# Layer 0's feed-forward for two entries between the state-space steps, C by DMA, sums over states by transposes, the last layer's second routing in front

## The chip, the cores and the metric

The kernel runs on one core of one Trainium2 chip. The metric is the device time of one execution in microseconds (us); lower is better. TensorE is written PE in profiles (PEld: its weight loads), VectorE DVE, ScalarE ACT, GpSimd POOL, SyncE SP. Before the change the median of three runs is 2589.24 us (2589.22 to 2589.57).

## The reference, cut to what matters

The reference is a decoder of four layers, each with self-attention, cross-attention and a feed-forward part, every part followed by a residual addition and a layer norm. There are four batch entries of 512 positions and 128 features, all in float32. The change touches three of the twelve parts:

```python
# L0_ffn: x is (4, 512, 128); _tlin multiplies by a matrix of -1, 0, 1 and scales
h = silu(_tlin(x, w1_w, w1_s)) * _tlin(x, w2_w, w2_s)      # 512 hidden features
h = gelu(_tlin(h, h1_w, h1_s), approximate=False)
h = gelu(_tlin(h, h2_w, h2_s), approximate=False)
return _tlin(h, w3_w, w3_s)                                # back to 128

# L1_attn: a selective state space, 256 inner features, 16 states
xi, z = split(x @ W_in);  xc = silu(conv4(xi) + conv_b)
dt, Bm, Cm = split(xc @ W_x, [8, 24])
delta = softplus(dt @ W_dt + b_dt);  A = -exp(A_log)
dA = exp(delta[..., None] * A);  dBu = delta[..., None] * Bm[:, :, None, :] * xc[..., None]
# over positions t: h = dA_t * h + dBu_t;  y_t = sum over the 16 states of h * C_t
return (y + xc * D) * silu(z) @ W_out

# L3_ffn: a shared expert for every row, and two of seven routed experts
probs = sigmoid(x @ Wr * routing_bias);  scores, idx = top_k(probs, 2)
out = shared(x) + sum over the two of (silu(x @ wg) * (x @ wu)) @ wd * score
```

## The kernel before

**The frame.** Each of the twelve parts is a generator that emits instructions and yields after every small piece. It has three phases: a start, up to the mark READY; a main phase, up to the mark TAIL; and a tail. While the main phase of a part runs, weights of the next part are loaded. Then the tail of the ending part (called "A") and the start of the next one (called "B"; for the parts in BESIDE also its first main pieces) are taken in turns, in an order written out by hand as a string of As and Bs in ORDER; when a string ends, the turns go on as "ABB". Nothing moves instructions after that: each engine does its instructions in the order in which they were emitted, and waits on semaphores for data and for buffers. So an instruction that waits holds up everything behind it on its engine.

**PSUM.** PSUM has a pool "s" of two tiles of two banks, and single banks "y", "v", "a0", "a1". A dictionary for each part and phase (RINGS: FORWARD for L0_ffn, STATES for L1_attn) says which of them a kind of use takes, in turn. A bank is free for its next writer when its last reader is done.

**L0_ffn** (from L1626). For each entry, `gates` does two matmuls of 128x512 for each of four chunks into a pair of banks; ACT applies silu, DVE multiplies the second result by its scale and by silu. `hidden` does four matmuls for each of four output chunks and a GELU on ACT, twice (layers h1 and h2). `output` does sixteen matmuls of 128x128, DVE multiplies by the scale, POOL adds the residual, and `finish_pieces` gives statistics (DVE, then two small POOL operations, L342 and L343), norm (DVE, L351) and the turning over into xT (four transposes, L359, and a copy). The start holds gates and h1 of entry 0. The main phase does everything else up to h1 of entry 3. The tail holds output of entry 2, h2 and output of entry 3, in turns with the start of L1_attn.

**L1_attn** (from L2284). The features lie on the 128 partitions in two halves c, positions along the row. `prepare(b)` gives the pieces for an entry: `convolved` (four shifted matmuls of 128x512 into pscv, silu to xc), `gates` (psz, silu to sz), `selected` (px, copied as bf16 to bc, with the remainders of the rounding in its other rows), `exponentials` (pdt, then seven ACT operations) and `logarithm` (five DVE operations for each half), and two POOL operations for de and du. Then there are 32 steps g, eight for an entry, each for NQ = 2 of the 16 states. In one step:

- `decays(g+1)`: four ACT exponentials, da (L2412)
- `spread(g+1, "B", c)`: PE spreads two rows of B over all partitions into pb, one tile of "s" for each half (L2398); `spread(g+1, "C", c)`: one matmul into pc (L2404), copied by ACT to cs (L2405)
- `recurred(g)`: for both halves DVE multiplies pb by du in place (L2423); then for each half DVE scans over positions (L2426) and POOL multiplies hh by cs (L2430)
- `summed(g-1, c)`: PE adds the two states into acc, a bank for each half that is kept over the entry's eight steps, by two matmuls with the identity (L2439)

The order in a step is recurred, decays, then for each half summed and spread. From step 1 of an entry on, the pieces of the next entry's `prepare` run one in each step (Agenda `early`, between summed(c=0) and spread(c=0)), and its logarithms in steps 4 and 5. `outputs` finishes an entry: DVE adds D times xc to acc (yt, L2448), POOL multiplies by sz, PE projects by W_out (yps) seven steps later, and residual, statistics and norm follow.

**L3_ffn** (from L1918). Rows are sorted to experts in two groups, entries 0 and 1 and entries 2 and 3. `routing(b)` computes the scores (plog, sigmoid, and some twenty small DVE operations), `ranked` and `numbered` the places, `placing` writes the rows to DRAM in that order by indirect DMA, `load` fetches them, two blocks at a time. The main loop goes over blocks q of 128 rows: `gates` (psgu, L2144), `hidden_over` (ph), `down` (py) and an indirect DMA out. The routing of entry 2 stands in front of the loop; that of entry 3, the ranks and the placing of the second group run inside it, by an agenda: 

```python
agenda.add(0, routing(3))
agenda.add(6, [lambda: ranked(1), lambda: None, lambda: numbered(1)])
for i, f in enumerate(placing(1)):
    agenda.add(9 + 3 * i // 4, [f])
```

## Time and profile before

| | us |
|---|---|
| median of the runs | 2589.24 |
| profiled execution | 2600.57 |
| its span on the engines | 2598.9 |
| first scan of L1_attn | 545.62 |
| start of its last two scans | 805.84 |
| first block of L3_ffn's loop on PE | 2454.50 |

The profiled execution is 11.3 us (0.44%) over the median, so a sum in its times has to be scaled before it is set beside a median. A row of a group or of a timeline gives the start, the busy time, the engine, the line in the kernel, what is written and read, and in brackets the idle time ahead of it with the instruction that ended it. In PE's rows the last part of a group can overlap the next row: a matmul is counted until its result has drained, so differences of starts give the pace. "PEclk" is the granted TensorE clock as a share of full speed; it is 0.954 over the whole span.

### The profile page before, as it was taken

The numbers are of one execution on the slowest core, as the hardware profiler recorded it, in microseconds if no ns is written. First come the engines' busy times: TensorE is split into PE (matmuls) and PEld (weight loads), VectorE is DVE, ScalarE is ACT, GpSimd is POOL, SyncE is SP. The second block draws the span as 40 slices with busy tenths as digits, with TensorE's granted clock in tenths as the row PEclk, the third lists the DMA queues.
The fourth block names the chain that finished last, engine by engine and source line by source line (L and its number), as shares of the span: only waits on it lengthen the run. The fifth ranks groups of instructions, "written<-read, shape, count | busy, mean of one in ns | idle before, by whom it ended". The sixth has DMA issues, their size and how long they took to land.

```text
span 2598.9 us, 37485 instructions
## 1 busy us (share of the span) xinstructions
PE 2310.4 (89%) x13754; PEld 1109.1 (43%) x13754; DVE 1681.9 (65%) x3028; ACT 1243.8 (48%) x2537; POOL 1138.3 (44%) x1545
## 2 busy tenths in 40 slices
PE   5998879988877998999999999999889799999887
PEld 1333334433333443444444555555445333344565
DVE  6896961179998666565554655655767699666434
ACT  2776432277652444333232455555354387745323
POOL 2342430157676325555552444344336434231354
PEclk7999899999988999999999999999899699999999
DMA  5422314000003400000000000000300243130112
GB/s 146 136 72 69 105 32 50 0 1 0 1 4 87 150 7 7 1 1 1 1 1 1 8 8 13 1 13 13 106 21 1 61 110 89 57 123 13 37 59 77
DMA packets 97415, 109.34 MB, mean 42 GB/s; under 512 B 30992, under 2 KB 82960, under 8 KB 97232
## 3 DMA queue, kind: packets, MB, share of 16 engines
q1 hardware_dynamic: 92592, 99.31, 13.8%
q0 software_dynamic: 2432, 5.02, 0.5%
q10 hardware_dynamic: 2208, 2.62, 0.3%
q8 instruction: 109, 1.79, 0.3%
q14 instruction: 74, 0.61, 0.1%
HBM read 68.94 MB, written 41.44 MB: 42 GB/s over the span
## 4 chain that ended last, share of the span: by engine, by line
PE 61%; DVE 16%; ACT 9%; POOL 5%; issue 4%; DMA 3%; SPq 1%; another core or an unknown queue 0%; POOLq 0%; ACTq 0%; DVEq 0%
PE av L714 4%; PE psve L1305 4%; PE scc L1142 4%; PE yT L1348 3%; PE avc L1215 3%; PE ptc L1202 3%; PE psh L1653 3%; ACT pr L1176 3%; PE sc L675 2%; DVE top L972 2%; PE avx L1000 2%; PE psqk L1487 2%; PE psgu L2144 2%; PE st L691 2%; DVE top L679 2%
## 5 line engine op out<-in xcount | busy, mean ns | idle before, releaser
L1186 POOL TENSOR_TENSOR pr<-pr,zs 128x1024 f32<-128x1024 f32 x192 | 237.1, 1252 | 238.8 <-DVE zs L1183 209.8
L679 DVE TENSOR_REDUCE top<-sc 128x2 f32<-128x1024 f32 x256 | 300.9, 1217 | 44.1 <-PE sc L675 41.4
L700 ACT ACTIVATE pT<-st 128x512 f32<-128x512 f32 x512 | 276.2, 598 | 88.3 <-PE st L691 85.1
L1176 ACT ACTIVATE pr<-scc,nm 128x256 f32<-128x256 f32 (+3 forms) x384 | 198.2, 526 | 179.5 <-DVE nm L1164 100.8
L972 DVE TENSOR_REDUCE top<-scx 128x4 f32<-128x616 f32 x256 | 192.2, 794 | 84.7 <-PE scx L959 73.5
L978 ACT ACTIVATE pTx<-stx 128x512 f32<-128x512 f32 x256 | 139.2, 596 | 201.4 <-PE scx L959 135.9
L497 POOL CAST nmP<-top 128x16 bf16<-128x16 f32 x96 | 25.4, 265 | 365.3 <-DVE top L972 203.6
L1164 DVE TENSOR_REDUCE nm<-scc 128x2 f32<-128x1024 f32 (+3 forms) x128 | 102.4, 821 | 120.1 <-PE scc L1149 120.1
L2430 POOL TENSOR_TENSOR hh<-hh,cs 128x1024 f32<-128x1024 f32 x64 | 149.3, 2354 | 65.9 <-DVE hh L2426 44.5
L714 PE MATMUL av<-pT,vbuf 128*32 128x256 f32 x2048 | 162.8, 392 | 8.9 <-ACT avs L514 8.9
L1310 DVE TENSOR_TENSOR vtmp<-psve,gm 128x1024 f32<-128x1024 f32 x64 | 78.3, 1224 | 130.7 <-PE psve L1305 130.6
L1142 PE MATMUL scc<-k,q 64*128 64x512 f32 (+3 forms) x768 | 143.4, 471 | 7.4 <-DVE vtmp L1310 3.3
L2426 DVE TENSOR_TENSOR_SCAN hh<-da,pb 128x1024 f32<-128x1024 f32 x64 | 142.6, 2269 | 0.0
L1315 POOL TENSOR_TENSOR vtmp<-vtmp 128x512 f32<-128x512 f32 x60 | 76.0, 1266 | 151.8 <-DVE vtmp L1310 131.4
L1202 PE MATMUL ptc<-ident,pr 128*128 128x128 f32 x960 | 136.4, 280 | 6.1 <-POOL pr L1186 4.1
L1305 PE MATMUL psve<-w_L_ffn,xT 128*128 128x512 f32 x256 | 123.3, 605 | 17.4 <-ACT pr L1176 11.9
L675 PE MATMUL sc<-kP,qP 64*128 64x512 bf16 x512 | 105.8, 412 | 35.1 <-DMA qP<-far_q 16.3
L2439 PE MATMUL acc<-hh,ident 128*128 128x512 f32 x256 | 131.7, 640 | 3.1 <-DVE yt L2448 2.0
L1215 PE MATMUL avc<-pT,v 128*64 128x512 f32 (+3 forms) x768 | 131.4, 449 | 0.5 <-DVE pT L1538 0.5
L1348 PE MATMUL yT<-gT,w_L_ffn 128*128 128x512 f32 x256 | 125.3, 613 | 0.0
L1202 PEld LDWEIGHTS ptc<-ident,pr 128*128 128x128 f32 x960 | 103.0, 141 | 46.0 <-issue 20.1
L691 PE MATMUL st<-qP,kP 64*128 64x512 bf16 x512 | 105.8, 385 | 3.2 <-DVE xT L332 1.7
(466 smaller groups left out, 4902.9 us busy)
## 6 DMA issues: line engine op xcount, KB each, us to landing
qP<-far_q SPq DMA_DIRECT2D x24, 768.0 KB
w_L_ffn<-in_L_ffn SPq DMA_DIRECT2D x24, 512.0 KB
far_q<-part SPq DMA_DIRECT2D x44, 192.0 KB
qP<-far_q SPq DMA_DIRECT2D x24, 256.0 KB
far_q<-part SPq DMA_DIRECT2D x44, 128.0 KB
kP<-far_k SPq DMA_DIRECT2D x7, 768.0 KB
kP<-far_kc SPq DMA_DIRECT2D x16, 231.0 KB
w_L_attn<-in_L_attn SPq DMA_DIRECT2D x6, 512.0 KB
```

Of the source, the lines that this page charges most:

```text
L675: nc.tensor.matmul(sc[:, r, :], lhsT=m["q"][rows, 2 * j + gp, qt * P : (qt + 1) * P], rhs=m["k"][rows, 2 * j + gp, :], start=True, stop=True,)
L679: return lambda: nc.vector.tensor_reduce(top[:, qt, 2 * gp : 2 * gp + 2], sc, AX.X, ALU.max, negate=True)
L700: nc.scalar.activation(pT, st, AF.Exp)
L714: nc.tensor.matmul(m["av"][32 * g : 32 * g + 32, part], lhsT=m["v"][:, kt, 4 * j + g, :], rhs=weights_of[s, g][:, part], start=(kt == 0 an ...
L972: nc.vector.tensor_reduce(ops.maxima(a)[:, 2 * qp : 2 * qp + 2, 2 * gp : 2 * gp + 2].rearrange("p i r -> p r i"), sc, AX.X, ALU.max, negat ...
L1142: nc.tensor.matmul(sc[:, r, at : at + n], lhsT=q[rows, qt * P : n], rhs=k[rows, :n], start=(i == 0), stop=not self.by_pe, skip_group_check ...
L1176: nc.scalar.activation(pr[:, r, at:to], sc[:, r, at:to], AF.Exp, bias=nm[:, i, r : r + 1], scale=1.0 if self.by_pe else -1.0, accum_out=zs ...
L1186: nc.gpsimd.tensor_tensor(pr[:, :, at : at + n], pr[:, :, at : at + n], zs[:, i, :, None].to_broadcast([P, 2, n]), ALU.mult)
L1202: nc.tensor.transpose(pt[:, r, to : to + P], self.pr[u, p][:, r, lo : lo + P], ident)
L1215: nc.tensor.matmul(av[64 * r : 64 * r + 64, kt * P :], lhsT=v[:, kt, 64 * r : 64 * r + 64], rhs=self.pT[u, part][:, r, at : at + n], start ...
L1305: nc.tensor.matmul(ps[:, r, :], lhsT=src[:, t * P : (t + 1) * P], rhs=w["ve"][:, h * 512 : (h + 1) * 512], start=True, stop=True,)
L1348: nc.tensor.matmul(yTs[b], lhsT=oe[:, c, e, :], rhs=gT[:, i, :], start=(c == 0 and e == 0), stop=(c == NC - 1 and e == NE - 1),)
```

## The change

1. **L0_ffn.** Its main phase now ends with entry 1's h1 and entry 0's output. Its tail finishes entry 1 and then does entries 2 and 3 alone as pieces of one chunk: `single_gates`, `single_hidden`, `single_output`. They use the banks a0 and a1, ACT does the scaling copies, and POOL multiplies. Their buffers lie in a part of the weights' spare room and in a buffer "late". The string WITH_STATES in ORDER puts them between the steps of L1_attn; with "beside" set, a step yields three times, ahead of either spread and at its end. L1_attn writes its results in place over L0_ffn's.
2. **C.** `selected` writes its sixteen rows of C to DRAM (far_c), and every step loads two of them, spread over all partitions, into cs (512 KB, on SP's queue) one step ahead. The matmuls pc and their copies are gone.
3. **Sums over states.** `summed` adds into acc by four transposes of 128x128 per state (so acc holds the sum turned), `outputs` copies acc by ACT and, one step later, turns it back by eight transposes (pty) ahead of DVE's yt. The gates psz of an entry move to its own step 6.
4. **L3_ffn.** The routing of entry 3 and the ranks and numbers of the second group stand in front of the loop, its placing in steps 0 to 11 instead of 9 to 20.

```diff
@@ -1684,6 +1687,40 @@
...
+
+        spare = w["spare"][:, BESIDE_AT:]
+        late_h = late.tile([P, 4, S], F32, name="hl", bufs=1)
+        late_g = spare[:, : 4 * S].rearrange("p (c n) -> p c n", c=4)
+        late_s = [spare[:, (4 + i) * S : (5 + i) * S] for i in range(2)]
+
+        def single_gates(b, c):
+            ps = [psum_v("psl", at) for at in SINGLE]
+            for r, wt in enumerate((w["w1"], w["w2"])):
+                nc.tensor.matmul(ps[r], lhsT=wt[:, c * P : (c + 1) * P], rhs=xT[:, b, :], start=True, stop=True)
+            nc.scalar.activation(late_s[c % 2], ps[0], AF.Silu, scale=w["s1"][:, c : c + 1])
+            nc.scalar.activation(late_g[:, c, :], ps[1], AF.Copy, scale=w["s2"][:, c : c + 1])
+            nc.gpsimd.tensor_tensor(late_g[:, c, :], late_g[:, c, :], late_s[c % 2], ALU.mult)
+
+        def single_hidden(of, to, wt, ws, o, at):
+            wv = w[wt].rearrange("p (c o) -> p c o", c=4)
+            ps = psum_v("psl", at)
+            for c in range(4):
+                nc.tensor.matmul(ps, lhsT=wv[:, c, o * P : (o + 1) * P], rhs=of[:, c, :], start=(c == 0), stop=(c == 3))
+            nc.scalar.activation(to[:, o, :], ps, AF.Gelu, scale=w[ws][:, o : o + 1])
+
+        def single_output(b, of):
+            w3 = w["w3"].rearrange("p (c o) -> p c o", c=4)
+            yp, ys = psum_v("psl", "a0"), new["x"][:, b * NT : (b + 1) * NT, :]
+            for t in range(NT):
+                for c in range(4):
+                    nc.tensor.matmul(
+                        yp[:, t * P : (t + 1) * P], lhsT=of[:, c, t * P : (t + 1) * P], rhs=w3[:, c, :],
+                        start=(c == 0), stop=(c == 3),
+                    )
+            nc.scalar.copy(ys, yp.rearrange("p (t d) -> p t d", t=NT))
+            nc.gpsimd.tensor_tensor(ys, ys, w["s3"][:, None, :].to_broadcast([P, NT, D]), ALU.mult)
+            nc.gpsimd.tensor_tensor(ys, ys, xs[:, b * NT : (b + 1) * NT, :], ALU.add)
+            ends.extend(finish_pieces(b, ys, new, last, split=True))
 
@@ -1697,45 +1734,46 @@
...
-        left = []
-        for b in range(B - 1):
-            for f in layer2(b) + left + layer1(b + 1):
-                f()
-            if b == B - 2:
-                break
-            stats, norm, turn_over = output(b)
-            stats()
-            for c in range(4):
-                gates(b + 2, c)
-            norm()
-            left = [turn_over]
-            if b == 0:
-                list(mask)
+        for f in layer2(0) + layer1(1):
+            f()
+        stats, norm, turn_over = output(0)
+        stats()
+        norm()
+        list(mask)
         room.leave(1)
         yield TAIL
...
             for r in range(2):
-                hidden(B - 1, hids, outs, "h2", "h2s", "hc", oo, (r,), later)
+                hidden(1, hids, outs, "h2", "h2s", "hc", oo, (r,), later)
                 yield PIECE
-                if (oo, r) == (0, 1):
-                    turn_over()
-                    yield PIECE
         for f in later:
             f()
         yield PIECE
-        stats, norm, turn_over = output(B - 1)
-        room.leave()
+        stats, norm, turn_over = output(1)
         yield PIECE
         for f in (stats, norm, turn_over):
             f()
             yield PIECE
+        room.leave(1)
+        def begins(b):
+            return [lambda c=c: single_gates(b, c) for c in range(4)] if b < B else [lambda: None] * 4
+
+        work = begins(2)
+        for b in range(2, B):
+            then = begins(b + 1)
+            for o in range(4):
+                work.append(lambda o=o: single_hidden(late_g, late_h, "h1", "h1s", o, SINGLE[o == 1]))
+            for o in range(4):
+                work.append(lambda o=o: single_hidden(late_h, late_g, "h2", "h2s", o, SINGLE[o == 1]))
+            work += [lambda b=b: single_output(b, late_g), then[0]] + [lambda: ends.pop(0)()]
+            work += then[1:] + [lambda: ends.pop(0)()] * 2
+        for f in work:
+            f()
+            yield PIECE
+        room.leave()
 
     def l2_ffn(w, cur, new, last, room):
@@ -2228,7 +2266,7 @@
...
-        early += [(2, f) for f in routing(2)]
+        early += [(b, f) for b in GROUPS[1] for f in routing(b)] + [(3, lambda: ranked(1)), (3, lambda: numbered(1))]
@@ -2240,10 +2278,9 @@
...
         total, edge = len(items), blocks[0]
-        agenda.add(0, routing(3))
-        agenda.add(6, [lambda: ranked(1), lambda: None, lambda: numbered(1)])
         for i, f in enumerate(placing(1)):
-            agenda.add(9 + 3 * i // 4, [f])
+            agenda.add(3 * i // 4, [f])
+        unplaced = len(agenda)
@@ -2339,7 +2369,8 @@
...
                 rest = m["dt"] = one.tile([P, S], F32, tag="rest", name="rest")
-                nc.scalar.copy(rest[32 : 32 + R, :], px[32 : 32 + R, :])
+                nc.scalar.copy(rest[: 32 + R, :], px[: 32 + R, :])
+                nc.sync.dma_start(far_c[b], rest[NS : 2 * NS, :])
@@ -2380,29 +2411,35 @@
...
                     lambda: convolved(0), lambda: convolved(1), selected, lambda: exponentials(0),
-                    lambda: exponentials(1), lambda: (gates(0), gates(1)),
+                    lambda: exponentials(1),
...
 
-        def spread(g, kind, c):
+        def gates(b):
+            sz = made[b]["sz"] = one.tile([P, 2, S], F32, tag="sz", name="sz")
+            for c in range(2):
+                ps = psum_a("psz")
+                nc.tensor.matmul(
+                    ps, lhsT=w["w_in"][:, (2 + c) * P : (3 + c) * P], rhs=state_T[:, b, :], start=True, stop=True
+                )
+                nc.scalar.activation(sz[:, c, :], ps, AF.Silu)
+
+        def spread(g, c):
...
             m = made[b]
-            if kind == "B":
-                pb = psum2("pb")
-                m["B", j, c] = pb
-                for i in range(NQ):
-                    n = j * NQ + i
-                    nc.tensor.matmul(pb[:, i, :], lhsT=pick[:, n : n + 1].to_broadcast([P, P]), rhs=m["bc"], start=True, stop=True)
-                return
-            if c == 0:
-                m["C", j] = work[0].tile([P, NQ, S], F32, tag="cs", name="cs")
-            pc = psum_v("pc", "a0")
-            n = NS + j * NQ + c
-            nc.tensor.matmul(pc, lhsT=pick[:, n : n + 1].to_broadcast([P, P]), rhs=m["bc"], start=True, stop=True)
-            nc.scalar.copy(m["C", j][:, c, :], pc)
+            pb = m["B", j, c] = psum2("pb")
+            for i in range(NQ):
+                n = j * NQ + i
+                nc.tensor.matmul(pb[:, i, :], lhsT=pick[:, n : n + 1].to_broadcast([P, P]), rhs=m["bc"], start=True, stop=True)
+
+        def fetched(g):
+
+            b, j = divmod(g, steps)
+            cs = made[b]["C", j] = work[0].tile([P, NQ, S], F32, tag="cs", name="cs")
+            nc.sync.dma_start(cs, far_c[b][None, j * NQ : (j + 1) * NQ, :].to_broadcast([P, NQ, S]))
@@ -2436,19 +2473,29 @@
...
                 n = j * NQ + i
-                nc.tensor.matmul(
-                    m["acc"][c], lhsT=ident, rhs=m["h", j][c][:, i, :], start=(n == 0), stop=(n == NS - 1),
-                    skip_group_check=True,
-                )
+                for t in range(NT):
+                    nc.tensor.matmul(
+                        m["acc"][c][:, t * P : (t + 1) * P], lhsT=m["h", j][c][:, i, t * P : (t + 1) * P], rhs=ident,
+                        start=(n == 0 and t == 0), stop=(n == NS - 1 and t == NT - 1), is_transpose=True,
+                        skip_group_check=True,
+                    )
...
             for c in range(2):
-                nc.vector.scalar_tensor_tensor(
-                    yt[:, c, :], m["xc"][:, c, :], w["dd"][:, c : c + 1], m["acc"][c], ALU.mult, ALU.add
-                )
-            nc.gpsimd.tensor_tensor(yt, yt, m["sz"], ALU.mult)
+                nc.scalar.copy(yt[:, c, :], m["acc"][c])
+
+            def turned():
+                for c in range(2):
+                    pt = psum_a("pty")
+                    for t in range(NT):
+                        nc.tensor.transpose(pt[:, t * P : (t + 1) * P], yt[:, c, t * P : (t + 1) * P], ident)
+                    nc.vector.scalar_tensor_tensor(
+                        yt[:, c, :], m["xc"][:, c, :], w["dd"][:, c : c + 1], pt, ALU.mult, ALU.add
+                    )
+                nc.gpsimd.tensor_tensor(yt, yt, m["sz"], ALU.mult)
+
@@ -2495,11 +2542,13 @@
...
         decays(0)
+        fetched(0)
         for c in range(2):
-            spread(0, "B", c)
-            spread(0, "C", c)
+            spread(0, c)
...
             b, j = divmod(g, steps)
+            while due:
+                due.pop()()
@@ -2513,21 +2562,29 @@
...
                 decays(g + 1)
+                fetched(g + 1)
+            if j == 6:
+                early.add(g, [lambda b=b: gates(b)])
...
                     early.run(g)
+                if new.get("beside"):
+                    yield PIECE
                 if g + 1 < total:
-                    spread(g + 1, "B", c)
-                    spread(g + 1, "C", c)
+                    spread(g + 1, c)
...
                 pieces = outputs(b - 1)
-                if b < B:
-                    early.add(g + 7, pieces[:1])
-                    late.add(g + 7, [lambda two=pieces[1:3]: [f() for f in two]])
-                    late.add(g + 8, [lambda end=pieces[3:]: [f() for f in end]])
+                if b == B:
+                    pieces[0]()
+                    pieces = pieces[1:]
+                else:
+                    due.append(pieces[0])
+                    early.add(g + 7, pieces[1:2])
+                    late.add(g + 7, [lambda two=pieces[2:4]: [f() for f in two]])
+                    late.add(g + 8, [lambda end=pieces[4:]: [f() for f in end]])
@@ -2550,7 +2607,7 @@
...
-        dict(p=("s",), t=SINGLE, a=SINGLE), dict(p=("s", "s", "yv"), t=SINGLE, a=SINGLE), dict(p=("s",), t=SINGLE, a=SINGLE),
+        dict(p=("s",), t=SINGLE, a=SINGLE), dict(p=("s", "s", "yv"), t=SINGLE, a=SINGLE), dict(p=("s",), t=("a0",), a=("a0",)),
@@ -2561,8 +2618,16 @@
...
 
+    def step(*ns):
+        return "".join("B" + "A" * n for n in ns)
+
+    ROUND = 2 * step(1, 0, 0) + step(1, 1, 0) + 2 * step(1, 0, 0) + 2 * step(1, 1, 1) + "A"
+    WITH_STATES = (
+        "ABBABABABABBABAABAA" + "A" * 4 + step(1, 1, 0) + ROUND + step(2, 1, 0) + ROUND + step(2, 0, 0)
+    )
+
     ORDER = dict(
-        L0_xattn="BABBABABBBABBABA", L1_attn="BABBABBAABABBAAABBAABABAA", L1_xattn="BABBBABABABBBA",
+        L0_xattn="BABBABABBBABBABA", L1_attn=WITH_STATES, L1_xattn="BABBBABABABBBA",
```

## The prediction

> **What bounds the kernel now.** I read the page's busy shares and its chain first, then a table of windows for the stretches that the diff touches, then the groups of one stretch, then single engines in order of time.
>
> ```profile
> span 2598.9 us, 37485 instructions
> ...
> PE 2310.4 (89%) x13754; PEld 1109.1 (43%) x13754; DVE 1681.9 (65%) x3028; ACT 1243.8 (48%) x2537; POOL 1138.3 (44%) x1545
> ...
> PE 61%; DVE 16%; ACT 9%; POOL 5%; issue 4%; DMA 3%; SPq 1%; another core or an unknown queue 0%; POOLq 0%; ACTq 0%; DVEq 0%
> ```
>
> PE carries the whole, but not every stage:
>
> ```profile
> core 0: us, PE busy (x) PEld busy (x) DVE busy (x) ACT busy (x) POOL busy (x), PEclk, DMA share, GB/s
> ...
> 428.00:541.00 113.00, 108.56 (x320) 51.83 (x319) 26.91 (x63) 40.33 (x58) 15.73 (x16) 1.00 0.00 0
> 541.00:806.00 265.00, 216.82 (x581) 91.01 (x580) 251.05 (x205) 179.50 (x278) 189.69 (x105) 0.92 0.02 5
> ```
>
> From 428 to 541 layer 0's feed-forward keeps PE at 108.6 of 113 us while DVE is nearly free; from 541 to 806 the state-space steps keep DVE at 251 of 265, and PE has 48 us free. The change moves PE work from the first stretch into the second. What matters is whether PE's free time there lies where the work is put.
>
> ```profile
> L2426 DVE TENSOR_TENSOR_SCAN hh<-da,pb 128x1024 f32<-128x1024 f32 x63 | 140.4, 2269 | 0.0
> L2439 PE MATMUL acc<-hh,ident 128*128 128x512 f32 x244 | 126.2, 643 | 3.1 <-DVE yt L2448 2.0 <-POOL hh L2430 1.2
> ...
> L2423 DVE TENSOR_TENSOR pb<-du,pb 128x1024 f32<-128x1024 f32 x64 | 75.7, 1217 | 9.1 <-PE pb L2398 8.6 <-POOL du L2378 0.5
> ```
>
> DVE's idle time in these 265 us is 9.1 in front of the product, 8.6 of it waiting for PE's pb. A step without other work is two products and two scans. Where PE has a convolution in the step, DVE waits already:
>
> ```profile
> 628.98 4.46 DVE L2426 TENSOR_TENSOR_SCAN hh<-da,pb 128x1024 f32<-128x1024 f32 x2
> 633.63 1.23 DVE L2423 TENSOR_TENSOR pb<-du,pb 128x1024 f32<-128x1024 f32 x1 [0.19 <-PE pb L2398]
> 635.99 1.23 DVE L2423 TENSOR_TENSOR pb<-du,pb 128x1024 f32<-128x1024 f32 x1 [1.14 <-PE pb L2398]
> 637.13 4.46 DVE L2426 TENSOR_TENSOR_SCAN hh<-da,pb 128x1024 f32<-128x1024 f32 x2
> 641.50 2.33 DVE L2423 TENSOR_TENSOR pb<-du,pb 128x1024 f32<-128x1024 f32 x2
> 643.75 4.46 DVE L2426 TENSOR_TENSOR_SCAN hh<-da,pb 128x1024 f32<-128x1024 f32 x2
> ```
>
> Scan to scan is 643.75-637.13 = 6.62 us where nothing is added, 637.13-628.98 = 8.15 with a convolution.
>
> **Part 1, the start of the states: -50.7.** Output(0) ends at 427.9 as before. PE then had entry 2's gates; now it waits for entry 0's norm: by the rows after 427.97 (ys 0.7, POOL add 1.4, statistics 1.7, POOL 0.2+1.0, norm 1.1) that is done at 434.3, and transposes and copy (0.6+0.7) let the first convolution start at 435.5. PE's rows from there: two convolutions 6.9, four hidden pieces of 3.43, px 1.7, pdt 2x1.05; ACT's queue between (two silu, three px copies, twice the exponential group of about 4.7, three table loads of 1.28, four GELU) ends at 469.7; output(1) at 472.7; its norm, again about 7.2, at 479.9, in front of entry 2's gates on PE's queue (8x0.857). Then pb, ACT's table load and decays: first scan at 491.1. Before it was 545.6: -54.5. The feed-forward of entries 2 and 3 is 76 us of PE work by rows (24 and 16 matmuls per entry at 0.857, and 3.6), so the rest went to waits. The two PE waits (6.4, 7.2) leave a cold clock: after 2.50 us idle the trace shows
>
> ```profile
> 585.84 0.38 PE L2404 MATMUL pc<-bc,pick 128*128 128x512 bf16 x1 [2.50 <-ACT cs L2405]
> 586.58 1.45 PE L2352 MATMUL pdt<-rest,w_L_attn 8*128 8x512 f32 x2 [0.36 <-DVE ln L2374]
> 587.96 3.78 PE L2439 MATMUL acc<-hh,ident 128*128 128x512 f32 x4
> 591.53 1.06 PE L2398 MATMUL pb<-bc,pick 128*128 128x512 bf16 x2
> ```
>
> where acc x4 is 1.88 elsewhere: +1.9 for each, 3.8 in all. Bounds: -54.5 to -47 (twice that).
>
> **Part 2, the steps: +46.5, and +7 for the clock.** On PE a step loses pc (two of 0.215) and has the sums as 16 transposes (0.107 each by the norm's transposes, four in 0.43, near 0.95 a half) in place of 1.72 a half: 4.7 us become 2.8. A piece adds 3.43. PE's queue between the pb of one step's second half and the first half of the next is: pb 0.43, sum 0.95, convolution 3.43, piece 3.43, pb 0.43 and 0.4 for hand-overs, 9.1; the first pb may not start before the scan that frees its bank. DVE has 6.62 of work. I went through all steps in this way, queue by queue, with these rows (GELU 0.62, decays 4x0.64, table loads 1.28, hh 2.35), first without the change: 253.7 from the first scan to the last, against 260.2 in the trace, where 4.8 are the leftover statistics and norm of entry 3. With it I get 305.5. The excess over the old steps, first entry: 1.3; convolutions 1.8 and 1.4; step 3, px and two pieces, 4.7; steps 4 and 5, 1.0 together (the logs hid most already); step 6, 9.6; step 7, 3.3; sum 23.1. Step 6 in full: psz(0) starts when the logs free its only bank; ACT has a GELU, two table loads and four decays (0.7+2.6+2.5) in front of its silu; psz(1) waits for that, output(2) (3.57) stands behind it, then ACT's copy 0.6 and POOL's two 1.27: 14.6 us until DVE, which has only 6.6 of its own work and the statistics next in its queue, goes on: 8.0 idle, 1.6 for the statistics. Step 7 holds the norm (3.3). The second entry costs 27.8, as DVE also waits 6.9 for the turned sums: pty stands behind two pieces, and behind two ACT copies, themselves behind a GELU. Entries 3 and 4 without pieces: -1.2 and +1.6. Total +51.3, less the 4.8 that leave: +46.5. Bounds: +3 (DVE alone, below) and +70 (each of some 14 piece steps 1.7 longer).
>
> In that sum PE idles 3.3, 5.6 and 3.7 us in either entry; at 1.9 each 11 us, of which I take 7, as some have slack; 0 to 24 if pieces run slow for longer. [...]
>
> C's load: 512 KB a step, issued one step early, and its buffer is free when the hh two steps before is done; by the sum it may take 9 us unseen. The nearest row, 768 KB of qP, lands in 4.08, and the engines are idle in this stretch (share 0.02): nothing, up to +5 if it takes 12. ACT loses 1.2 us a step; the DRAM write is four times in all. 21 more table loads (1.28) are in the sum above.
>
> **Part 3, the end of the states: +1.5.** pty is queued behind the norm's four transposes (last at 818.01); then twice 0.5 on PE and 0.7 on DVE in one bank: 820.8 instead of 819.27. Bounds 0 and +3.
>
> **Part 4, the last layer: +4.** Routing(3), ranks and numbers now stand in front of psgu(0) at
>
> ```profile
> 2454.50 1.35 PE L2144 MATMUL psgu<-w_L_ffn,xb 128*128 x4
> ...
> 2457.30 1.28 ACT L1970 ACT_TABLE_LOAD   x1
> ...
> 2462.12 1.35 PE L2144 MATMUL psgu<-w_L_ffn,xb 128*128 x4
> ```
>
> In front: plog 0.9, sum 0.2, table load and sigmoid 1.5, 26 small DVE operations of about 0.2, rank matmul 0.6: +8.4. Behind, the gap between 2458.31 and 2462.12 loses its table loads, -2.4; later steps lose rank work and the 0.8 that PE waited for the placement at 2529.66, -0.6 to -3. Net +4, bounds 0 and +7. The other stages keep their order.
>
> **Sum.** -50.7+46.5+7+1.5+4 = +8.3 on the profiled execution's 2600.57 (11.3 above the median of 2589.24): 2608.9, by the same ratio 2597.5. No change can be told within 0.2%, 5.2 us.
>
> **Rivals.**
> - *The states stay bound by DVE* (faster). PE's work in them would be 32x2.8, 76 of pieces and about 48 for preparing: 212, under the 254 of DVE. If the queues slide past each other, part 2 is +3 and the whole about -42: 2547; with half of the waits gone, 2571. For it: the sum of the work fits. Against it: the trace shows DVE waiting for pb with one convolution already, and only four pb banks couple them. It decides below 84% of part 2's 53.5.
> - *The clock stays low* (slower): pieces and convolutions at half speed for half of 14 steps, +24: 2621. For it: 0.92 granted already, 3.78 above. Against: with the pieces PE's share of the stretch is not lower.
> - *C arrives late* (slower): only above 9 us; +5, 2602. Against it: idle DMA engines.
> - *The last layer hides its front* (same): with +0 in part 4, 2593.5.
>
> **How the numbers follow.** The lock step as summed, with or without the last layer's part: 0.48; clock or load worse: 0.24; waits partly or wholly gone: 0.28. Of the first, whose own range is 2585 to 2608, a quarter falls within 0.2% of before and a tenth below. So faster 0.28+0.05=0.33, within 0.2% 0.12, slower 0.31+0.24=0.55. The range, with about 0.1 left out on either side, is 2562 to 2625.
>
> **What would show it.** First scan near 491 to 495 (part 1). The product's idle time, 9.1 before, at 40 or more with pb as its releaser, and waits of 8 us for POOL's ys and 7 for pty on DVE (part 2). A granted clock below 0.92 in the steps. yt of entry 3 about 1.5 later after the last scan. psgu(0) 8 us later after the last ype, and fewer waits behind it. The prediction is wrong if DVE is at 95% in the steps with pieces, or if scans wait for hh's C.

## The result, and the profile after

The changed kernel takes 2599.78 us in the median of five runs (2596.02 to 2605.94); the kernel before, in five runs beside it, 2589.24 (2587.19 to 2591.70). The ratio is 1.0047 with an interval of [1.0034, 1.0061], so it is slower by 12 us (the two medians are 10.5 apart). The forecast was 2597.5. The total was close, but its terms were not all right: the gain of part 1 was put too high, the costs of parts 2 and 3 too low, and part 4 had the wrong sign.

The profiled execution after took 2599.71 us, almost the 2600.57 of the one before. Do not read this as "no change": the last layer alone is 13 us shorter in the trace after than in the trace before, and by the experiments below a step of that size goes with the chip and not with the edit (experiment 9). What can be compared is the start of the program, stage by stage. First the page of the changed kernel: busy shares, the chain, and the DMA row of C.

```profile
span 2598.0 us, 37923 instructions
...
PE 2265.8 (87%) x13953; PEld 1135.3 (44%) x13978; DVE 1677.3 (65%) x3018; ACT 1247.4 (48%) x2512; POOL 1150.5 (44%) x1555
...
PE 61%; DVE 17%; ACT 9%; POOL 6%; issue 4%; DMA 2%; SPq 1%; ACTq 0%; POOLq 0%; DVEq 0%
...
cs<-far_c SPq DMA_DIRECT2D x32, 512.0 KB, 3.7
```

Nothing of the bound has changed over the whole span: PE carries 61% of the chain, as before. C's 32 loads land in 3.7 us, far below the 9 us from which, by the prediction's sum, they would have cost time. The table of windows shows more:

```profile
core 0: us, PE busy (x) PEld busy (x) DVE busy (x) ACT busy (x) POOL busy (x), PEclk, DMA share, GB/s
428.00:541.00 113.00, 88.09 (x271) 44.08 (x273) 51.47 (x62) 60.89 (x83) 43.94 (x32) 0.89 0.09 29
541.00:806.00 265.00, 187.84 (x785) 116.88 (x798) 213.21 (x190) 155.48 (x219) 164.25 (x92) 0.84 0.16 55
```

Before, each stretch had one engine that was full: PE with 108.6 of 113 us, then DVE with 251 of 265. Now no engine is full in either. In the second stretch DVE has 52 us free and PE 77: they wait for each other. And the granted clock, 0.92 before, is 0.84. Where DVE waits, by what ended the wait (total, times, longest):

```profile
DVE st L340 <- POOL x L1722: 19.6, 2, 10.2
DVE pb L2460 <- PE pb L2436: 19.3, 12, 3.5
DVE pb L2460 <- PE psl L1699: 10.1, 1, 10.1
DVE yt L2494 <- ACT yt L2487: 9.9, 1, 9.9
DVE yt L2494 <- PE pty L2493: 7.4, 5, 2.9
```

The third line is a single wait ahead of the first scan. The other four are 56 us of idle DVE in the steps, where the trace before has 11 in all, 8.6 of them for pb. The first and the fourth line are two that the prediction had worked out: the statistics of the piecewise output, which stand in DVE's queue and wait for POOL's residual, and the turned sums. In DVE's rows in order of time, a step with a convolution and one piece, and then steps 6 to 8 of the first entry:

```profile
516.69 4.46 DVE L2463 TENSOR_TENSOR_SCAN hh<-da,pb 128x1024 f32<-128x1024 f32 x2
523.72 2.53 DVE L2460 TENSOR_TENSOR pb<-du,pb 128x1024 f32<-128x1024 f32 x2 [2.57 <-PE pb L2436]
526.16 4.46 DVE L2463 TENSOR_TENSOR_SCAN hh<-da,pb 128x1024 f32<-128x1024 f32 x2
...
559.51 4.46 DVE L2463 TENSOR_TENSOR_SCAN hh<-da,pb 128x1024 f32<-128x1024 f32 x2
574.20 0.29 DVE L340 BATCH_NORM_STATS2 st<-x 128x6 f32<-128x128 f32 x1 [10.23 <-POOL x L1722]
...
578.05 4.46 DVE L2463 TENSOR_TENSOR_SCAN hh<-da,pb 128x1024 f32<-128x1024 f32 x2
...
589.79 4.45 DVE L2463 TENSOR_TENSOR_SCAN hh<-da,pb 128x1024 f32<-128x1024 f32 x2
604.14 0.75 DVE L2494 SCALAR_TENSOR_TENSOR yt<-xc,w_L_attn,pty 128x512 f32<-128x512 f32 x1 [9.90 <-ACT yt L2487]
...
608.71 4.46 DVE L2463 TENSOR_TENSOR_SCAN hh<-da,pb 128x1024 f32<-128x1024 f32 x2
```

A convolution step is 9.47 us long (526.16-516.69; 8.15 before). Step 6 is 18.54 (578.05-559.51), step 8 is 18.92. What PE did in front of the wait of step 6, and in front of the first steps:

```profile
434.79 1.15 PE L360 MATMUL pt<-ident,x 128*128 128x128 f32 x4 [5.71 <-DVE x L352]
439.38 5.11 PE L2359 MATMUL pscv<-xT,taps 128*128 128x512 f32 x8 [3.43 <-POOL taps L2333]
...
447.75 3.59 PE L2359 MATMUL pscv<-xT,taps 128*128 128x512 f32 x8
...
472.93 5.72 PE L1679 MATMUL yp<-w_L_ffn,hc 128*128 128x128 f32 x32 [7.28 <-ACT hc L1661]
484.35 1.15 PE L360 MATMUL pt<-ident,x 128*128 128x128 f32 x4 [5.70 <-DVE x L352]
486.28 9.49 PE L1699 MATMUL psl<-xT,w_L_ffn 128*128 128x512 f32 x16 [0.78 <-DVE xT L333]
...
563.95 2.08 PE L2424 MATMUL psz<-xT,w_L_attn 128*128 128x512 f32 x2 [5.43 <-ACT sz L2427]
565.82 5.05 PE L1716 MATMUL psl<-w_L_ffn 128*128 128x128 f32 x32
```

A float32 matmul of the kernel stands as two in these rows (a transpose as one), so x8 are the four matmuls of a convolution. They take 5.11 us after an idle stretch and 3.59 eight microseconds later. The windows of the two show the clock:

```profile
core 0: us, PE busy (x) PEld busy (x) DVE busy (x) ACT busy (x) POOL busy (x), PEclk, DMA share, GB/s
439.40:444.40 5.00, 5.00 (x9) 2.26 (x10) 0.00 (x0) 0.00 (x0) 0.00 (x0) 0.71 0.01 3
447.80:451.30 3.50, 3.50 (x10) 1.60 (x9) 0.00 (x0) 0.00 (x0) 0.00 (x0) 1.00 0.00 0
```

Below, "warm" means at a granted clock of 1.00, and "cold" means less. The waits of PE in these rows are paid twice: once as a wait, and once more as cold matmuls behind it (behind the wait of 3.43 us, 5.11 us against 3.59). The last two rows of PE are the chain that was foreseen for step 6: psz(1) behind ACT's silu, and the output behind psz(1).

By stage, in starts of rows in the two traces (a top-k is a row of DVE that writes `top`):

| us | before | after | difference | predicted |
|---|---|---|---|---|
| first scan | 545.6 | 499.2 | -46.4 | -50.7 |
| first to last scan | 260.2 | 319.0 | +58.8 | +46.5 and +7 |
| last scan to the next layer's first top-k | 21.2 | 25.4 | +4.2 | +1.5 |
| from there to the last layer | 1562.0 | 1557.9 | -4.1 | 0 |
| last layer, from the last top-k to the end | 209.8 | 196.5 | -13.3 | +4 |

The first three rows add up to +16.6. The last row differs between chips as much as between kernels, which experiments 1, 2 and 9 are for; the row above it is 1556 to 1562 us in all fourteen traces, whatever the kernel.

### The profile page after: what moved, and what is told of

Same layout as the page of the kernel before. It is cut to its first block, busy times and chain, and to the rows that moved or that the text cites. A ratio compares the mean times of both kernels' runs of the same rounds, so it can differ in the third digit from the quotient of the medians.

```text
span 2598.0 us, 37923 instructions
## 1 busy us (share of the span) xinstructions
PE 2265.8 (87%) x13953; PEld 1135.3 (44%) x13978; DVE 1677.3 (65%) x3018; ACT 1247.4 (48%) x2512; POOL 1150.5 (44%) x1555
## 4 chain that ended last, share of the span: by engine, by line
PE 61%; DVE 17%; ACT 9%; POOL 6%; issue 4%; DMA 2%; SPq 1%; ACTq 0%; POOLq 0%; DVEq 0%
PE av L715 4%; PE psve L1306 4%; PE scc L1143 4%; PE yT L1349 3%; PE avc L1216 3%; PE ptc L1203 3%; ACT pr L1177 3%; PE sc L676 2%; DVE top L973 2%; PE psgu L2182 2%; PE psqk L1488 2%; PE avx L1001 2%; PE st L692 2%; DVE top L680 2%; PE psl L1708 2%
## 5 line engine op out<-in xcount | busy, mean ns | idle before, releaser
L498 POOL CAST nmP<-top 128x16 bf16<-128x16 f32 x96 | 25.4, 265 | 362.2 <-DVE top L973 202.2
L1306 PE MATMUL psve<-w_L_ffn,xT 128*128 128x512 f32 x256 | 123.5, 607 | 17.3 <-ACT pr L1177 11.9
L676 PE MATMUL sc<-kP,qP 64*128 64x512 bf16 x512 | 106.1, 413 | 36.0 <-DMA qP<-far_q 16.6
L960 PE MATMUL scx<-kP,qP 64*128 64x154 bf16 x1024 | 86.7, 242 | 25.6 <-DVE top L973 14.7
```

Of the source, the lines that this page charges most:

```text
L676: nc.tensor.matmul(sc[:, r, :], lhsT=m["q"][rows, 2 * j + gp, qt * P : (qt + 1) * P], rhs=m["k"][rows, 2 * j + gp, :], start=True, stop=True,)
L1306: nc.tensor.matmul(ps[:, r, :], lhsT=src[:, t * P : (t + 1) * P], rhs=w["ve"][:, h * 512 : (h + 1) * 512], start=True, stop=True,)
```

## The experiments

Experiments 1 to 4 ran on one chip, 5 to 8 on a second, 9 to 12 on a third, each with its own runs of the kernel before, whose medians there were 2589.69, 2603.65 and 2601.73 us. Absolute times are compared within a chip, ratios across chips. "Steps" is the time from the first to the last scan, "tail" that from there to the next layer's first top-k.

**1. The change without part 4** (the last layer's routing as it was).

```diff
-        early += [(b, f) for b in GROUPS[1] for f in routing(b)] + [(3, lambda: ranked(1)), (3, lambda: numbered(1))]
+        early += [(2, f) for f in routing(2)]
...
+        agenda.add(0, routing(3))
+        agenda.add(6, [lambda: ranked(1), lambda: None, lambda: numbered(1)])
         for i, f in enumerate(placing(1)):
-            agenda.add(3 * i // 4, [f])
+            agenda.add(9 + 3 * i // 4, [f])
```

> The changed kernel with its fourth part undone: entry 3's routing, the ranks and the second group's placing are back inside the last layer's loop. By the prediction, the fourth part costs 4 us (0 to 7): this run 4 us below the changed kernel, about 2596 us, first block of the loop about 9 us earlier after entry 2's last sum. The rival, suggested by the two profiles (the last layer took 13 us less in the changed kernel's profile than in that of before): the part pays for itself, and this run is 5 to 13 us above the changed kernel, 2605 to 2613.

Measured: 2606.24 us, ratio 1.0062 [1.0040, 1.0084], which is +16 us, the +16.6 of the first three stages, and not the 2596 us that a part 4 of +4 would give. Its steps took 319.2. Its first scan, at 502.4, comes 46.6 us ahead of experiment 2's on the same chip, where layer 0 is as before.

**2. Part 4 alone**, on the kernel before (the same lines the other way round).

> The kernel before with the fourth part alone. Prediction: 4 us slower than before (0 to +7), 2593. Rival: 5 to 13 us faster than before, 2576 to 2584. If the 13 us between the two profiles were a peculiarity of one profiled execution, it is within 5 us of before either way.

Measured: 2584.99 us, ratio 0.9992 [0.9977, 1.0007]. Alone it makes no difference that can be told, with its middle on the side of a gain. On this chip the front, from the last top-k to the first block, took 55.7 us with the old routing (experiment 1) and 63.2 with the new, +7.5; from the first block to the end of the kernel it took 140.4 and 128.9, -11.5. The front's +8.4 was sized about right. The loop gives back far more than the 3 to 5.4 us that I had put there. How much it is hangs on the chip, by single traces: on the second chip the loop to the end took 145.2 us with the old routing (experiment 8) and 138.4 to 140.1 with the new (experiments 5 to 7), 5 to 7 less, and the layer as a whole did not gain. Part of the 11.5 is seen in experiment 1's waits of PE in the last layer, which experiment 2's don't have; the rest I have not divided up:

```profile
PE pxs L2161 <- DMA sb<-far_s: 6.3, 4, 2.8
```

**3. The lighter steps alone**: C by DMA, the sums by transposes and psz in step 6, without moving any feed-forward work (on the changed kernel, parts 1 and 4 taken back; one line of that is shown).

```diff
-        L0_xattn="BABBABABBBABBABA", L1_attn=WITH_STATES, L1_xattn="BABBBABABABBBA",
+        L0_xattn="BABBABABBBABBABA", L1_attn="BABBABBAABABBAAABBAABABAA", L1_xattn="BABBBABABABBBA",
```

> The kernel before with the second and third part alone: C by DMA, sums by transposes, psz at the entry's own step 6; the feed-forward stays where it was, the last layer too. If PE's and ACT's load is what DVE waits for in the steps, the 9.1 us of waits for pb shrink by 5 to 8 and the end costs 1.5: 2582 to 2587. If the transposes let the clock fall, the granted clock in the steps is below 0.92 and the time is at 2590 or above. If C comes late, POOL's product waits for cs and the time is above 2592.

Measured: 2593.01 us, ratio 1.0017 [1.0001, 1.0034]; steps 262.6 and tail 25.8, against 260.2 and 21.2 before. The granted clock in them is 0.82. What was to make room on PE makes the steps themselves no shorter.

**8. C by DMA alone**, on the kernel before; told here because it is the other half of experiment 3.

```diff
-            pc = psum_v("pc", "a0")
-            n = NS + j * NQ + c
-            nc.tensor.matmul(pc, lhsT=pick[:, n : n + 1].to_broadcast([P, P]), rhs=m["bc"], start=True, stop=True)
-            nc.scalar.copy(m["C", j][:, c, :], pc)
+        def fetched(g):
+            b, j = divmod(g, steps)
+            cs = made[b]["C", j] = work[0].tile([P, NQ, S], F32, tag="cs", name="cs")
+            nc.sync.dma_start(cs, far_c[b][None, j * NQ : (j + 1) * NQ, :].to_broadcast([P, NQ, S]))
```

> The kernel before with C by DMA alone: no pc matmul, no copy, sums and all else as before. Less work on PE and ACT and no transposes: the convolution steps lose 0.4 of 1.4 us waits, 2584 to 2590, granted clock at 0.90 or more. If the load of C is what costs in the run with both lighter parts, POOL waits for cs in the last entry and the time is 2592 to 2596.

Measured: 2595.86 us, ratio 0.9970 [0.9955, 0.9985]; steps 255.0, tail 22.1. So C by DMA is a gain of 0.3%, and the transposes with the moved psz, which are what experiment 3 has beyond it apart from the places of a few buffers, lose 0.47% (1.0017/0.9970, from two chips). In the starts of the scans the loss lies in four places: the steps 8, 16 and 24, where a finished entry is turned back, are 2.1, 3.8 and 3.0 us longer in experiment 3, and the last step, behind the last entry's psz, 2.7; elsewhere it gains 4.0. The windows of two stretches late in the steps, experiment 8 first, then experiment 3:

```profile
core 0: us, PE busy (x) PEld busy (x) DVE busy (x) ACT busy (x) POOL busy (x), PEclk, DMA share, GB/s
680.00:765.00 85.00, 67.87 (x169) 27.86 (x170) 82.28 (x72) 45.46 (x68) 60.39 (x33) 0.91 0.16 56
765.00:810.00 45.00, 34.99 (x95) 14.34 (x96) 41.17 (x36) 12.96 (x21) 36.78 (x26) 0.96 0.33 89
```

```profile
680.00:765.00 85.00, 58.57 (x244) 37.77 (x249) 77.51 (x69) 45.67 (x68) 56.11 (x28) 0.77 0.16 56
765.00:810.00 45.00, 29.97 (x148) 22.27 (x151) 41.60 (x27) 16.50 (x26) 34.48 (x24) 0.81 0.31 87
```

With the sums as matmuls the clock is granted at 0.91 and 0.96, with transposes at 0.77 and 0.81. The rows do not show whether the transposes themselves are the reason, because PE is also less busy with them (58.6 of 85 us against 67.9).

**7. The changed kernel with its sums as matmuls again.**

```diff
+                nc.tensor.matmul(
+                    m["acc"][c], lhsT=ident, rhs=m["h", j][c][:, i, :], start=(n == 0), stop=(n == NS - 1),
+                    skip_group_check=True,
+                )
```

> The changed kernel with its sums over states by the matmuls of before, everything else as changed. By PE's queue, 1.5 us more work in each of the first 17 steps: +10 to +25, 2610 to 2625. Against that stand the wait for the turned sums (6.9 and 9.9 us seen in the first two entries' ends) and the clock: if the transposes are what let it fall to 0.84 in the steps, it is at 0.90 or more here and the run is within 8 us of the changed kernel, 2592 to 2608.

Measured: 2616.44 us, ratio 1.0048 [1.0035, 1.0061], the changed kernel's own ratio. The steps took 318.8 against 319.0, but by entries 95.0, 100.4, 69.4, 53.9 against 90.6, 98.3, 71.8, 58.3: the transposes save 6.5 us in the two entries that carry pieces and lose 6.8 in the two that don't (3.6 and 6.2 by experiment 9's trace of the changed kernel). From 680 to 810 us the clock is granted at 0.92 in this kernel and at 0.76 to 0.79 in the changed one. The low clock is real, but trading it back for longer sums gains nothing in all. Step by step, the transposes save 1.6 to 3.2 us in each step that holds a convolution or px, where PE is overfull. In the last two entries the loss lies in the steps 16 and 24, where a finished entry is turned back: 15.9 and 14.7 us against 11.4 and 12.3, 6.9 in all. So there it is the turning back that costs; the steps that take 6.6 us in experiment 7 take 6.6 to 7.0 under the low clock.

**4. Entry 3's feed-forward alone as pieces**, entry 2's done ahead as before: half of the work, spread over 16 steps.

```diff
-        work = begins(2)
-        for b in range(2, B):
...
+        b = B - 1
+        work = [lambda c=c: single_gates(b, c) for c in range(4)]
...
-        "ABBABABABABBABAABAA" + "A" * 4 + step(1, 1, 0) + ROUND + step(2, 1, 0) + ROUND + step(2, 0, 0)
+        "BABBABBAABABBAAABBAABABABA" + 2 * step(0, 0, 0) + step(1, 0, 0) + 2 * step(1, 1, 0) + step(0, 1, 0)
+        + 2 * step(1, 0, 0) + 3 * step(0, 0, 0) + 2 * step(1, 1, 0) + step(0, 1, 0) + step(0, 0, 1) + step(1, 0, 1)
```

> The changed kernel with only entry 3's feed-forward as pieces between the steps, and entry 2's where it was, so that 38 us of PE work are spread over 16 steps instead of 76 (none in a step with a convolution, the output two steps ahead of its statistics). If the loss comes from PE's queue being too full in the first 16 steps and from the waits at the output, the first scan is at 508 to 515, the steps from first to last scan take 262 to 275 instead of 319, DVE's wait for POOL's residual is below 2 us, and the time is 2558 to 2575, below both kernels. If the loss is a fixed price of the interleaving (clock, table loads, DMA), the steps take over 300 and the time is above 2590.

Measured: 2596.72 us, ratio 1.0027 [1.0014, 1.0040]; first scan 504.5, steps 310.1. That is a miss: half of the pieces lengthen the steps by 47.5 us over experiment 3, all of them by 56.4. PE's rows in steps 4 and 5 of the first entry show part of the reason:

```profile
537.33 1.02 PE L1699 MATMUL psl<-xT,w_L_ffn 128*128 128x512 f32 x2
545.78 2.07 PE L1699 MATMUL psl<-xT,w_L_ffn 128*128 128x512 f32 x2 [7.43 <-DVE du L2415]
...
555.40 1.02 PE L1699 MATMUL psl<-xT,w_L_ffn 128*128 128x512 f32 x2
563.85 2.08 PE L1699 MATMUL psl<-xT,w_L_ffn 128*128 128x512 f32 x2 [7.42 <-DVE du L2415]
```

The second half of a gate piece writes bank a1, and a1 holds pdt until DVE's logarithm has read it. My turns had put gate pieces into just the two steps that have logarithms. PE, which does its queue in order, stands 7.4 us with the next pb behind it.

**5. The same pieces in other places**: the gates ahead of step 4, and the hidden pieces in a0 only.

```diff
-            work.append(lambda o=o: single_hidden(late_g, late_h, "h1", "h1s", o, SINGLE[o == 1]))
+            work.append(lambda o=o: single_hidden(late_g, late_h, "h1", "h1s", o, "a0"))
...
-        "BABBABBAABABBAAABBAABABABA" + 2 * step(0, 0, 0) + step(1, 0, 0) + 2 * step(1, 1, 0) + step(0, 1, 0)
-        + 2 * step(1, 0, 0) + 3 * step(0, 0, 0) + 2 * step(1, 1, 0) + step(0, 1, 0) + step(0, 0, 1) + step(1, 0, 1)
+        "BABBABBAABABBAAABBAA"
+        "BBABBBABBAABABAABBABBBABBABBBBBBABBBABBBABBBBBBABBBABBBBABBABBBABABBBB"
```

> As the run with entry 3 alone as pieces, and only their places are others: all four gate pieces ahead of step 4, the hidden pieces all in bank a0, one a step, the output two thirds of a step ahead of its statistics. If the 48 us that the run before lost in its steps came from where the pieces stood (gate pieces in steps 4 and 5 waited 7.4 us for bank a1, which the logarithms hold), the steps from first to last scan take 278 to 295 instead of 310 and the time is 2565 to 2582. If every piece costs its price wherever it stands, they stay above 300 and the time at 2590 or more.

Measured: 2590.57 us, ratio 0.9954 [0.9938, 0.9969]; steps 283.3, first scan 504.8. The same work in other places takes the steps from 310.1 to 283.3, and the kernel is faster than before. So feed-forward work does fit between the steps in part, in this quantity and in chosen places. Of the 26.8 us, 12.0 are gained in the first entry, where the two waits for a1 (14.9 us) stood, and 11.9 in the second, which had no gate pieces: the other moves count as much, and no run takes them apart.

**6. Experiment 5 with matmul sums for the last two entries**, and the last entry's psz in its step 2.

```diff
+                if b >= 2:
+                    nc.tensor.matmul(
+                        m["acc"][c], lhsT=ident, rhs=m["h", j][c][:, i, :], start=(n == 0), stop=(n == NS - 1),
+                        skip_group_check=True,
+                    )
+                    continue
...
-            if j == 6:
+            if j == (2 if b == B - 1 else 6) and b < B:
```

> As the run beside it, with the sums of entries 2 and 3 by the matmuls of before (no pieces run there), and psz of entry 3 at step 2 of its entry. If transposes let the clock fall, the granted clock after 690 us is at 0.90 or more instead of 0.77 to 0.83, the last seven steps take 6.6 each and the end from the last scan to the next stage is 4 us shorter: 5 to 12 us below the run beside it, 2555 to 2575. If the clock follows PE's idle time alone, it stays within 0.03 and the gain is 3 to 5 us, of psz and of the end.

Measured: 2586.70 us, ratio 0.9936 [0.9915, 0.9957]. The tail is 22.4 against 25.9, the steps are the same (283.8): psz, now in step 2 of the last entry, makes that step 10.2 long. The granted clock from 745 to 795 us is 0.96 against 0.88. The intervals of 5 and 6 overlap, so the gain of 6 over 5 is read from the tail alone. It had been expected at 5 to 12 us if the clock rose; the clock rose, and the gain is 3.9.

**9. The changed kernel once more**, on the chip of experiments 10 to 12, as what they are compared with.

> The changed kernel as it is, on the chip of the three runs beside it: 1.003 to 1.006 times before.

Measured: 2621.86 us, ratio 1.0072 [1.0053, 1.0091], its middle over what was expected; steps 321.4. Its last layer, from the last top-k to the end, took 214.7 us against 196.5 in the first trace of this same kernel. DVE's waits there hold one that the first trace lacks, and the trace of the kernel before has it too:

```profile
DVE ys L2141 <- remote: 7.3, 1, 7.3
```

"remote" is the profile's word for a release it cannot place. The other traces say the same: on the first chip (experiments 1 to 4) the layer took 192 to 196 us with either routing and has no such wait on DVE, on the two others (experiments 5 to 12) it took 211 to 215 with either routing and always has one at ys, of 5.8 to 9.5 us. So the 13 us that the two first traces seemed to say for part 4 go with the chip; their cause stays open.

**10. Statistics later**: the statistics of a piecewise output behind all gate pieces of the next entry, so that DVE's queue does not hold them while POOL is late.

```diff
-            work += [lambda b=b: single_output(b, late_g), then[0]] + [lambda: ends.pop(0)()]
-            work += then[1:] + [lambda: ends.pop(0)()] * 2
+            work += [lambda b=b: single_output(b, late_g)] + then + [lambda: ends.pop(0)()] * 3
```

> The changed kernel with the three other gate pieces of the next entry between single_output and its statistics, instead of the statistics in front of them. If the 9 to 10 us that DVE waits for POOL's residual add in step 6 are a loss of their own, steps 6 to 8 of the first two entries shrink by 6 to 9 us in each, 12 to 18 us in all. If PE's queue in these steps (psz with its wait for ACT, output, gates) is as long as DVE's wait, the sum of steps 6 to 8 changes by less than 4 us in each entry, and only the place of the wait moves.

Measured: 2612.41 us, ratio 1.0049 [1.0033, 1.0066]; steps 316.7. Steps 6 to 8 took 16.2, 17.4 and 15.6 us, where experiment 9 has 18.7, 10.8 and 22.7: 3.0 less in sum. The interval overlaps experiment 9's. DVE's rows show the wait in two new places:

```profile
560.17 4.46 DVE L2462 TENSOR_TENSOR_SCAN hh<-da,pb 128x1024 f32<-128x1024 f32 x2
572.17 1.23 DVE L2459 TENSOR_TENSOR pb<-du,pb 128x1024 f32<-128x1024 f32 x1 [7.55 <-PE pb L2435]
...
590.42 1.11 DVE L352 TENSOR_SCALAR x<-x,mvf,rsf 128x128 f32<-128x128 f32 x4 [8.05 <-POOL rsf L344]
```

With the statistics gone, DVE waits 7.55 us for the next thing that PE owes it, pb. The 10 us wait "for POOL" in step 6 is PE's queue, as it stands behind psz(1) and the output; POOL was only the last link. The second wait, for POOL's rsf, ends a longer chain: in POOL's queue rsf stands behind the product of the last gate piece (587.86 us), which waited for ACT's copies of what PE computed at 583.53, after PE had waited 2.75 us for ACT.

**11. psz split**: of every entry, psz(0) in step 6 and psz(1) in step 7.

```diff
-            if j == 6:
-                early.add(g, [lambda b=b: gates(b)])
+            if j == 6 and b < B:
+                early.add(g, [lambda b=b, c=c: gates(b, c) for c in range(2)])
```

> The changed kernel with the two psz of an entry in steps 6 and 7 instead of both in step 6, so that the second does not stand in PE's queue waiting for ACT's silu of the first. By the working of step 6 (psz(1) waits 5.6 us, and output, copy and residual follow it), step 6 shrinks by 5 to 6 us in each of the first two entries, and step 7 grows by 1 to 3: 4 to 10 us less in all. If another wait takes its place, less than 2.

Measured: 2607.41 us, ratio 1.0025 [1.0009, 1.0041], clear of experiment 9's interval; steps 310.4, 11.0 less than in experiment 9. Step 6 is 13.8 long against 18.7, step 14 is 13.9 against 18.5, and the last step 6.6 against 8.0. DVE's rows of step 6:

```profile
559.39 4.46 DVE L2463 TENSOR_TENSOR_SCAN hh<-da,pb 128x1024 f32<-128x1024 f32 x2
569.38 0.29 DVE L340 BATCH_NORM_STATS2 st<-x 128x6 f32<-128x128 f32 x1 [5.53 <-POOL x L1722]
```

The wait is 5.53 us instead of 10.23. One wait of PE for one ACT silu, in front of a long piece, was worth about 5 us in each of two steps.

**12. Experiment 6 with psz split** and entry 3's turning over later.

```diff
-                early.add(g, [lambda b=b: gates(b)])
+                early.add(g, [lambda b=b, c=c: gates(b, c) for c in range(2)])
...
-        "BBABBBABBAABABAABBABBBABBABBBBBBABBBABBBABBBBBBABBBABBBBABBABBBABABBBB"
+        "BBABBBABBAABABAABBABBBABBABBBBBBABBBABBBABBBBBBABBBABBBBABBABBBABBBABB"
```

> The run with entry 3's pieces placed and matmul sums for entries 2 and 3, with psz split as in the run beside it, and xT of entry 3 two thirds of a step later. Steps of 278 to 283 us from first to last scan instead of 283.8, 0.990 to 0.994 times before; above 0.9955 if the split only moves the waits.

Measured: 2581.33 us, ratio 0.9923 [0.9908, 0.9938], faster than both kernels. Steps 282.8, tail 22.1. Step 6 fell from 11.1 to 6.7, but step 23 is 13.0 where it was 8.9, so the steps as a whole gain only 1.0 over experiment 6, whose interval overlaps this one.

## Why the prediction was right, and where its terms were off

**Part 1, -50.7; measured -46.4**, outside its bounds (-54.5 to -47) by 0.6. Two things were mis-sized. The first convolution began at 439.4 instead of 435.5, because PE waited 3.43 us for POOL's tap matrices, which was not in the sum; ACT's queue, and with it output(1), came 3.2 late by that. And I took 3.8 for the cold clock by two restarts at 1.9 us. There were more: by the rows above against the warm ones, the convolution lost 1.5 (5.11 against 3.59), the output 2.0 (5.72 against 3.73), the gates 2.5 (9.49 against some 7.0 at 16 matmuls), the two groups of transposes 0.6 each. 7 us in place of 3.8. (The row that the 1.9 came from stands behind 2.50 us of idle PE, and the granted clock there is 0.50 from 588 to 592 us.) The two do not simply add up, as the cold convolution is in the 3.2: from the 491.1 of the sum without a clock to the measured 499.2 it is 8.1, 3.2 up to output(1) and 4.9 behind it.

**Part 2, +46.5 and +7; measured +58.8.** By entries I had +18.3 (23.1 less the 4.8 that leave), +27.8, -1.2 and +1.6; measured were +21.9, +31.4, +0.7 and +4.8. The sum without a clock was thus 12.3 short, and 7 had been put down for the clock. (The excesses listed add up to 51.3, while 305.5 less 253.7 is 51.8: a slip of 0.5.) Single steps are near: steps 0 to 2 together at +6.0 (4.5 predicted), step 3 at +4.6 (4.7), steps 4 and 5 at +1.3 (1.0), step 6 at +9.6 (9.6). The wait for POOL's residual was 10.23 and 9.41 us, not 8.0, and that for the turned sums 9.90, not 6.9. Its rows show cold pieces in that chain: the matmuls of a hidden piece (x8) took 5.40 us behind PE's wait of 4.00 for xT, at a granted clock of 0.67, where they take 3.60 warm. Step 7 came out at +5.1 (3.3). The last entry's excess was not foreseen: its psz, moved to step 6, now stands in PE's queue among the last steps; PE waits 3.14 us for ACT between its halves, and the last step is 9.3 us long. With psz split, in experiment 11, it is 6.6.

**The mechanism of part 2 holds**: the steps run in lock step with PE's queue. The product and the statistics waited with PE and POOL named as releasers, as said; experiments 10 and 11 show which one it was. Taking the statistics out moved the wait onto pb; taking out what PE waits for shortened it. Of the signs that had been named, the waits for POOL and for the turned sums and a clock below 0.92 came; the product's idle time in the steps is 22 us (19.3 and 2.7), not the 40 or more that had been named.

**Part 3, +1.5; measured +4.2**, over its bound of +3. pty's two groups took 1.12 and 1.09 us instead of the 0.5 that I took for each, with waits of about 1 us ahead of either. With matmul sums the tail is 21.6 (experiment 7) and 22.1 (experiment 8).

**Part 4, +4; measured about -2** where it ran alone beside the kernel before: experiment 2 gives 0.9992, with an interval that holds no change, and the changed kernel's 1.0047 stands beside 1.0062 without part 4, whose intervals overlap. The front's +8.4 came out at +7.5. The term that failed is what the loop gives back: 11.5 us on the first chip and 5 to 7 on the second, in place of 3 to 5.4. The rival "the last layer hides its front" described this better, though what pays for it is not the cover of the front but the loop.

So errors of +4.3, +5.3, +2.7 and about -6 come to +6: 8.3 predicted would be 14 to 15, and the runs say 12.2 (8.8 to 15.8). The forecast was right in sign and mechanism, and near in size by luck, because part 4's error paid for the others.

**The rivals.** "Bound by DVE" is refuted for this change: its condition was below 84% of the 53.5 us, and it was 110%. (Its PE work adds up to 214, not 212.) For half of the work it is not true either, but the work pays: in experiment 5 entry 3's pieces lengthen the steps by 20.7 us over experiment 3 (283.3-262.6) and bring the first scan forward by 40.4. "C arrives late" is refuted: it lands in 3.7 us, POOL waits 1.0 us for it in all, and experiment 8 is a gain. "The clock stays low" spoke of the steps with pieces, and there it did not come: the changed kernel's clock is 0.93 from 499 to 600 us and 0.89 from 600 to 690, beside 0.92 in the steps before. It is low (0.78 and 0.80) in the last two entries, which have no pieces and are only 5.5 us longer. And in experiment 7 a higher clock, bought with longer sums, left the ratio where it was.

**Where the gain went.** Moving both entries' feed-forward brings the first scan forward by 46 us and lengthens the steps by 56.4 over experiment 3; moving one, in good places, -40.4 and +20.7. So the second half of the work brings the first scan forward by only 6 us more and costs 36 in the steps. The reason that I see, which no run tests by itself: entry 2's result is due at its convolution early in the second entry, so its pieces have only eight steps, and entry 3's the next eight. C by DMA gains 0.3%, transposes and the moved psz lose 0.47%.

Not settled: what in the last layer's loop gains 11.5 us on one chip and 5 to 7 on another, beyond the 6.3 of waits for sb; why that layer takes some 19 us longer on two of the chips; and whether the clock falls with transposes because of their kind or because PE idles more.

## What to carry to other kernels

When a profile shows one engine free in a stage and another stage's work is moved there, do not add up busy times: ask in which steps the work must be done, which bank it writes and who reads that bank last. The same pieces, 38 us of PE work by the prediction's sum, made the kernel slower by 0.27% or faster by 0.46%, depending on their places and banks; two waits of 7.4 us for a bank that a slow reader held were the largest part that the rows show. When a wait names an engine, look at what that engine was waiting for itself before moving the waiting instruction.

## What was not expected of the hardware

- The same kernel differs by chip: the kernel before had medians of 2589.7, 2603.7 and 2601.7 us on three chips, and the last layer took 192 to 196 us in four traces on the first and 211 to 215 in eight on the others, there with a wait on DVE of 5.8 to 9.5 us that the profile calls "remote". A difference between two single traces in that stage says nothing unless they are of one chip.
- Behind four waits of PE, of 3.43, 4.00, 5.70 and 7.28 us, the next long group of matmuls took 1.5 to 2.5 us longer than warm (5.11 against 3.59, 5.40 against 3.60, 9.49 against some 7.0, 5.72 against 3.73), on top of the wait, at granted clocks of 0.67 to 0.80; behind one of 3.48 us, at 580.39, the clock was 1.00. I had counted only two such restarts in part 1, at 1.9.
- A broadcast load of 512 KB over 128 partitions in every step, at a DMA share of 0.16, cost nothing that shows (POOL waited 1.0 us for it in all) and was worth 0.3% in experiment 8.
